# Two neighbouring weight rows to a partition, larger load pieces, and VectorE's extra jobs given out step by step, in an LSTM with a binary feed-forward net

## The chip, the cores and the metric

The kernel runs on one core of one Trainium2 chip. The metric is device time in microseconds; a run's time is taken around the whole execution. The profile shows one execution, by engine: TensorE (PE, with PEld for its weight loads), VectorE (DVE), ScalarE (ACT), GpSimd (POOL), SyncE (SP), and the DMA queues.

## The reference

x is 32 x 64 x 256 (sequences, steps, features), `cond` is 32 x 256, all f32. An LSTM runs over the 64 steps, a net with weights of +1 and -1 follows, and x is added:

```python
xW = jnp.einsum('ntd,dg->ntg', x, Wx) + b          # Wx 256 x 1024
a = xw_t + prev_h @ Wh                             # Wh 256 x 1024, one step
i, f, o = sigmoid(a[:, :256]), sigmoid(a[:, 256:512]), sigmoid(a[:, 512:768])
g = tanh(a[:, 768:])
next_c = f * prev_c + i * g
next_h = o * tanh(next_c)
# over all steps: hs, then, with w(k) = where(k, 1, -1)
h = relu(s0 * concat([hs, -hs]) @ w(k0)) * 2       # k0 512 x 1024
h = relu(s1 * h @ w(k1)) * 2                       # k1 1024 x 1024
out = x + s2 * h @ w(k2)                           # k2 1024 x 256
```

## The kernel before

**Layout.** The 256 hidden units are cut into four quarters q of 64. A partition holds (q, n): quarter q of sequence n, 4 x 32 = 128 partitions, so that the cell's elementwise work is 64 wide. Matmuls contract over 128 rows and take a step's x or h turned, 32 columns of sequences; their outputs go to the four quarters of the partitions, and four such matmuls run side by side. The 256 rows of Wx, Wh and of each half of k0 are two chunks of 128 partitions: row (q, b, j) lies in partition (q, j) of chunk b, j from 0 to 31. To match it, a transposition by 32 x 32 blocks on VectorE turns x (`turn_x`, line 214) and h (line 311).

**x products.** `x_part` (228 to 237) computes for one step and chunk the x share of the gates, and `x_products` (254) does two steps to a PSUM bank: eight calls of four matmuls each, and each f32 matmul is two matmul instructions in the profile. `evict_x` (242) adds the bias on VectorE and stores the bank to `xg`. `next_x` (247) turns the next eight steps of x and asks for the load of eight steps further on. The first eight steps are done in pieces, as their data come in, then steps 8 to AHEAD - 1 (here 12), and only then step 0 of the recurrence.

**A step** (lines 477 to 495): `gates_from_h` (273) multiplies h by Wh; `cell_step` (291) does the sigmoids and tanh on ScalarE and `kept`, `new`, `c`, `h` and the transposition to `hist` on VectorE, and copies the next step's `xg` into PSUM (ScalarE, 288 and 289). Behind that in program order come a step's share of other PE work and the chores. Each engine works in the order of the program. In steps 0 to X_STEPS - 1 (0 to 20) the PE work is x products, afterwards the feed-forward net of blocks of 16 steps (`ffn_block`, 373), shared evenly by a `goal`. The chores, one a step from step FIRST_CHORE (4) on, make the +1/-1 weights: four of `make_w0` (ScalarE and then VectorE, 190), eight of `make_w1` (ScalarE, 198), four of `make_w2` (ScalarE, 202). After every fourth step `split_h` (316) splits four steps' h into a high and a low part, on ScalarE (`hhi`) and VectorE (`hlo`).

**Loads.** SyncE and ScalarE share the first loads, in this order: four steps of x, Wx for f and o (chunk 0, then chunk 1), four steps of x, Wx for g, Wx for i, eight steps of x (half 1), Wh for g, Wh for i, f and o. Each is cut into four transfers of 32 partitions, two to a queue (`load_gates`, 109). Behind them SyncE alone loads x halves 2 and 3, k0 (eight transfers), k1 and further x. GpSimd loads the bias, `cond` and the scales.

Of the kernel before, what the change touches and what calls it, by code (L numbers as in the profile page):

```python
# [38 lines left out]
def lstm_ffn(ctx: ExitStack, tc: tile.TileContext, x, cond, wx_d, wh_d, b_d, k0_d, k1_d, k2_d, s0_d, s1_d, s2_d, out):  # L39
    nc = tc.nc  # L40
    P = 128
    N, T, D = x.shape
    H = cond.shape[1]
    G = 4 * H
    NQ = 4
# [4 lines left out]
    SB = 16  # L50
    NB = T // SB
    TB = SB * N
    SH = 4

    GATES = (3, 0, 1, 2)

    AHEAD = 12
    X_STEPS = 21

    FIRST_CHORE = 4  # L60
    WARM_UP = 8

    const = ctx.enter_context(tc.tile_pool(name="const", bufs=1))
# [15 lines left out]
    xq = {}  # L79
# [26 lines left out]
    def rows(t, q):  # L106
        return t[q * 32 : (q + 1) * 32]

    def load_gates(t, w_d, slots, engines, chunks=slice(0, 2)):

        w_rows = w_d.rearrange("(q b j) g -> q j b g", q=NQ, b=2)
        s0, n, g0 = slots[0], len(slots), GATES[slots[0]]
        for q in range(NQ):
            engines[q % len(engines)].dma_start(
                out=rows(t, q)[:, chunks, s0 * H : (s0 + n) * H],
                in_=w_rows[q, :, chunks, g0 * H : (g0 + n) * H],
            )

    load_x(0, 0, [nc.sync, nc.scalar], slice(0, SB // 4))
# [15 lines left out]
    h_first = const.tile([P, HQ], F32, name="h_first")  # L135
    nc.gpsimd.dma_start(out=h_first, in_=cond.rearrange("n (q j) -> q n j", q=NQ))
    scales = []
    for i, s_d in enumerate((s0_d, s1_d, s2_d)):
        s = const.tile([P, 1], F32, name=f"s{i}")
# [2 lines left out]
    load_x(1, 0, [nc.sync])  # L142
    load_x(1, 1, [nc.sync])

    k0_rows = k0_d.rearrange("(s q b j) g -> s q j b g", s=2, q=NQ, b=2)
    k0_bits = []
    for i in range(2):
        t = act([P, 2, F0], U8, f"k0_{i}")
        for q in range(NQ):
            nc.sync.dma_start(out=rows(t, q), in_=k0_rows[i, q])  # L150
        k0_bits.append(t)


# [48 lines left out]
    def make_w2(k, m):  # L202
        nc.scalar.activation(
            w2[:, m, ts(k, 4)].rearrange("p k (q j) -> p k q j", q=NQ),
            bits[FC0 + k].rearrange("p (k q m j) -> p m k q j", k=4, q=NQ, m=2)[:, m],
            AF.Identity,
            bias=minus1,
            scale=2.0,
        )


    xT = {}

    def turn_x(i, half, part=slice(0, SB // 2)):
        if part.start == 0:
            xT[i, half] = act([P, SB // 2, 2, N], F32, f"xT{i}_{half}")
        nc.vector.transpose(  # L217
            xT[i, half][:, part].rearrange("p t b n -> p (t b n)"),
            xq[i, half][:, part].rearrange("p t j -> p (t j)"),
        )  # L220

    wx_q = wx.rearrange("p k (g q j) -> p k q g j", g=4, q=NQ)
    wh_q = wh.rearrange("p k (g q j) -> p k q g j", g=4, q=NQ)
    xg = {}

    def x_part(p, t, k, slots, start):

# [14 lines left out]
    def evict_x(p, t):  # L242
        xg[t] = gpool.tile([P, 2, 4 * HQ], F32, tag="xg", name=f"xg{t}")
        b = bias[:, :4].rearrange("p g j -> p (g j)").unsqueeze(1).to_broadcast([P, 2, 4 * HQ])
        nc.vector.tensor_tensor(xg[t], p.rearrange("p t g j -> p t (g j)"), b, ALU.add)  # L245

    def next_x(half):

        if half < 2 * NB:
            turn_x(*divmod(half, 2))  # L250
            if half + 4 < 2 * NB:
                load_x(*divmod(half + 4, 2), [nc.sync])

    def x_products(t0, t1):

        for t in range(t0, t1, 2):
            p = x_bank(t)
            for s in range(2):
                for k in range(2):
                    x_part(p, t + s, k, slice(0, 4), s == 0 and k == 0)  # L260
                    if s == 1 and k == 1:
                        evict_x(p, t)
                        half, left = divmod(t + 2, SB // 2)
                        if left == SB // 4 and t + 2 != AHEAD:
                            next_x(half + 1)
                    yield 2


# [4 lines left out]
    def gates_from_h(t, hT):  # L273
        for g, slots in zip(gates, (slice(0, 3), slice(3, 4))):
            for k in range(2):
                for q in range(NQ):
                    nc.tensor.matmul(  # L277
                        g[q * N : (q + 1) * N],
                        hT[:, k, :],
                        wh_q[:, k, q, slots],  # L280
                        start=False,
                        stop=(k == 1),
                        skip_group_check=True,
                    )
# [6 lines left out]
    def cell_step(t, c):  # L291
        sig = cell.tile([P, 3, HQ], F32, tag="sig", name=f"sig{t}")
        cand = cell.tile([P, HQ], F32, tag="cand", name=f"cand{t}")
        nc.scalar.activation(sig[:, 0:2, :], gates[0][:, 1:3], AF.Sigmoid)  # L294
        nc.scalar.activation(cand, gates[0][:, 0], AF.Tanh)  # L295
        nc.scalar.activation(sig[:, 2, :], gates[1][:, 0], AF.Sigmoid)  # L296
        kept = cell.tile([P, HQ], F32, tag="kept", name=f"kept{t}")
        nc.vector.tensor_mul(kept, sig[:, 1, :], c)  # L298
        new = cell.tile([P, HQ], F32, tag="new", name=f"new{t}")
        nc.vector.tensor_mul(new, sig[:, 0, :], cand)  # L300
        c = cell.tile([P, HQ], F32, tag="c", name=f"c{t}")
        nc.vector.tensor_add(c, kept, new)  # L302
        th = cell.tile([P, HQ], F32, tag="th", name=f"th{t}")
        nc.scalar.activation(th, c, AF.Tanh)  # L304
        h = cell.tile([P, HQ], F32, tag="h", name=f"h{t}")
        nc.vector.tensor_mul(h, sig[:, 2, :], th)  # L306
        i, s = divmod(t, SH)
        if s == 0:
            hist[i] = hpool.tile([P, 2, SH * N], F32, tag="hist", name=f"hist{i}")
        hT = hist[i][:, :, ts(s, N)]  # L310
        nc.vector.transpose(hT, h.rearrange("p (b j) -> p b j", b=2))  # L311
        if t + 1 < T:
            gates_from_x(t + 1)
        return c, hT
# [135 lines left out]
    for t in range(SB // 2):  # L450
# [3 lines left out]
            evict_x(banks[t // 2], t - 1)  # L454
        if t == 1:
            turn_x(0, 1)
    nc.vector.transpose(hT, h_first.rearrange("p (b j) -> p b j", b=2))
    for _ in x_products(SB // 2, AHEAD):
        pass
    gates_from_x(0)  # L460
# [7 lines left out]
    chores = deque()  # L468
    chores += [lambda k=k, h=h: make_w0(k, h) for k in range(2) for h in range(2)]
    chores += [lambda k=k: make_w1(k) for k in range(FC0)]  # L470
    chores += [lambda k=k, m=m: make_w2(k, m) for k in range(2) for m in range(2)]

    work = x_products(AHEAD, T)
    total_x = (T - AHEAD) * 4
    total_ffn = (NB - 1) * (4 * FC0 + 2 * FC0 * FC1 + 4 * FC1)
    done = 0
    for t in range(T):
        gates_from_h(t, hT)
        c, hT = cell_step(t, c)
        if t == 0:  # L480
            next_x(AHEAD // (SB // 2) + 1)
        later = chores.popleft()() if t >= FIRST_CHORE and chores else None
        if outputs and next(outputs[0], "end") == "end":
            outputs.popleft()
        if t == X_STEPS:
            work, done = ffn(), 0
        goal = (t + 1) * total_x // X_STEPS if t < X_STEPS else (t + 1 - X_STEPS) * total_ffn // (T - X_STEPS)
        while done < goal:
            done += next(work)
        if t == X_STEPS - 1:  # L490
            next(work, None)
        if callable(later):
            later()
        if t % SH == SH - 1:
            split_h(t // SH)
    for n, _ in enumerate(work):
        if outputs and n % 4 == 0 and next(outputs[0], "end") == "end":
            outputs.popleft()
# [28 lines left out]
```

## Time and profile before

| what | value |
|---|---|
| median of four runs | 319.12 us (318.32 to 319.89) |
| the profiled execution's own time | 319.49 us |
| its span, from the first to the last instruction | 317.7 us |
| mean granted TensorE clock | 0.998 |
| start of the gate matmuls of step 0 | 19.58 us |
| start of the gate matmuls of step 21 | 84.00 us |
| an x turn, 128x512 (line 217) | 698 ns |
| an eviction of x products, 128x512 (line 245) | 662 ns |
| the product h, 128x64 (line 306) | 226 ns |
| h turned to hist, 128x64 (line 311) | 246 ns |

The page of a profile gives each engine's busy time, the span in 40 slices, and the chain of work that ended last, followed back from the end. The timeline merges neighbouring instructions of a kind: the columns are start, length, engine, line, operation, output <- input, count, and in brackets the idle time before with what ended it. A wait for several semaphores is put down to the one that came last by the profile. SPq and ACTq are transfers issued by SyncE and ScalarE; their rows show the issue, not the transfer.

### The profile page before, as it was taken

Reading aid. Unit: us, or ns where it says so; the run is one execution under the profiler, and the core shown is the slowest. Engines: PE = TensorE matmul, PEld = TensorE weight load, DVE = VectorE, ACT = ScalarE, POOL = GpSimd, SP = SyncE. Lnnn points to the kernel's source line nnn. Section 1 sums busy time; section 2 is a strip of 40 time slices with the busy share of each in tenths; the row PEclk is TensorE's granted clock in tenths of the full one; section 3 lists DMA queues with packets and bytes.
Section 4 is the critical chain, followed back from the end, with each engine's and each line's share of the span. In section 5 each row is a group of like instructions: output and inputs, shape, how many; then the busy total and the mean of one; then the engine's idle time right before and its main releaser. Section 6 shows DMA issues by size and latency. Waiting matters only on the chain.

```text
span 317.7 us, 9440 instructions
## 1 busy us (share of the span) xinstructions
PE 307.2 (97%) x3978; PEld 235.1 (74%) x3978; DVE 153.7 (48%) x473; ACT 130.8 (41%) x484; POOL 9.2 (3%) x28
## 2 busy tenths in 40 slices
PE   7889999999999999999999999999999999999992
PEld 4767777777877777777777777777777777888881
DVE  1355886756674433335745434467443433811114
ACT  0214567875563433344633334355334432511111
POOL 4400000000000000000000000000000000000001
PEclk9999999999999999999999999999999999999999
DMA  5665401142000000000010000001310000220002
GB/s 142 180 134 152 89 2 42 46 110 47 5 0 2 2 0 2 3 0 2 2 34 23 14 1 2 2 0 32 71 34 3 2 0 2 66 66 2 0 0 66
DMA packets 31001, 10.99 MB, mean 35 GB/s; under 512 B 28072, under 2 KB 30376, under 8 KB 30960
## 3 DMA queue, kind: packets, MB, share of 16 engines
q1 hardware_dynamic: 27648, 8.66, 11.3%
q10 hardware_dynamic: 3040, 1.57, 1.9%
q8 instruction: 31, 0.51, 0.7%
q0 software_dynamic: 272, 0.17, 0.3%
q14 instruction: 10, 0.08, 0.1%
HBM read 8.29 MB, written 2.10 MB: 33 GB/s over the span
## 4 chain that ended last, share of the span: by engine, by line
PE 88%; DMA 6%; DVE 3%; issue 1%; ACT 1%; DVEq 0%; ACTq 0%
PE p L407 38%; PE gates L277 19%; PE px L230 12%; PE p L379 10%; PE po L392 9%; DMA x<-in_x_dram 3%; DMA wx<-in_L_cond_Wx_dram 2%; DMA wh<-in_L_cond_Wh_dram 1%; DVE xg L245 1%; DVE w L194 0%; ACT th L304 0%; DVE h L306 0%; DVE c L302 0%; DVE o L362 0%; DVE hist L311 0%
## 5 line engine op out<-in xcount | busy, mean ns | idle before, releaser
L277 PEld LDWEIGHTS gates<-wh,hist 128*32 128x32 f32 x2016 | 54.3, 109 | 25.4 <-issue 14.1
L277 PE MATMUL gates<-wh,hist 128*32 128x192 f32 x2016 | 68.1, 275 | 0.4 <-DVE hist L311 0.3
L230 PE MATMUL px<-wx,xT 128*32 128x256 f32 (+1 forms) x1152 | 61.1, 357 | 1.5 <-DMA x<-in_x_dram 0.8
L294 ACT ACTIVATE sig<-gates 128x128 f32<-128x128 f32 x64 | 17.8, 278 | 81.4 <-PE gates L277 81.1
L230 PEld LDWEIGHTS px<-wx,xT 128*32 128x32 f32 x1152 | 40.2, 111 | 13.9 <-DVE xT L217 1.5
L298 DVE TENSOR_TENSOR kept<-sig,c 128x64 f32<-128x64 f32 x63 | 14.1, 224 | 59.5 <-ACT sig L294 59.2
L304 ACT ACTIVATE th<-c 128x64 f32<-128x64 f32 x64 | 16.5, 257 | 31.3 <-DVE c L302 31.3
L379 PE MATMUL p<-hhi,w 128*128 128x512 f32 x64 | 25.5, 399 | 0.0
L379 PE MATMUL p<-hlo,w 128*128 128x512 f32 x64 | 25.3, 395 | 0.0
L306 DVE TENSOR_TENSOR h<-sig,th 128x64 f32<-128x64 f32 x64 | 14.5, 226 | 20.7 <-ACT th L304 20.7
L245 DVE TENSOR_TENSOR xg<-px,bias 128x512 f32<-128x512 f32 x32 | 20.9, 662 | 5.1 <-POOL sgn L158 3.9
L288 ACT COPY gates<-xg 128x192 f32<-128x192 f32 x64 | 20.0, 313 | 0.0
L311 DVE STREAM_TRANSPOSE hist<-h 128x64 f32<-128x64 f32 x64 | 15.7, 246 | 2.4
L302 DVE TENSOR_TENSOR c<-kept,new 128x64 f32<-128x64 f32 x64 | 14.4, 225 | 2.2
L296 ACT ACTIVATE sig<-gates 128x64 f32<-128x64 f32 x64 | 14.9, 232 | 0.0
L379 PEld LDWEIGHTS p<-hhi,w 128*128 128x128 f32 x64 | 12.0, 188 | 2.8
L300 DVE TENSOR_TENSOR new<-sig,cand 128x64 f32<-128x64 f32 x64 | 14.0, 218 | 0.0
L295 ACT ACTIVATE cand<-gates 128x64 f32<-128x64 f32 x64 | 14.0, 218 | 0.0
L379 PEld LDWEIGHTS p<-hlo,w 128*128 128x128 f32 x64 | 12.0, 188 | 2.6
L407 PE MATMUL p<-a_7h,w 128*128 128x512 f32 x32 | 13.0, 407 | 0.0
L289 ACT COPY gates<-xg 128x64 f32<-128x64 f32 x64 | 13.0, 203 | 0.0
L407 PE MATMUL p<-a_2l,w 128*128 128x512 f32 x32 | 12.9, 403 | 0.0
(121 smaller groups left out, 500.0 us busy)
## 6 DMA issues: line engine op xcount, KB each, us to landing
x<-in_x_dram SPq DMA_DIRECT2D x58, 64.0 KB, 2.5
out_dram<-o SPq DMA_DIRECT2D x28, 64.0 KB, 1.8
bits<-in_L_ffn_k_dram SPq DMA_DIRECT2D x10, 128.0 KB, 2.3
wx<-in_L_cond_Wx_dram SPq DMA_DIRECT2D x8, 64.0 KB, 2.5
wx<-in_L_cond_Wx_dram ACTq DMA_DIRECT2D x8, 64.0 KB, 2.8
k<-in_L_ffn_k_dram SPq DMA_DIRECT2D x8, 64.0 KB, 3.0
wh<-in_L_cond_Wh_dram SPq DMA_DIRECT2D x2, 192.0 KB, 4.1
wh<-in_L_cond_Wh_dram ACTq DMA_DIRECT2D x2, 192.0 KB, 5.1
```

The lines of the kernel that those rows point to most:

```text
L230: nc.tensor.matmul(p[q * N : (q + 1) * N, t % 2, slots], xT[i // 2, i % 2][:, s, k, :], wx_q[:, k, q, slots], start=start, stop=False, ski ...
L245: nc.vector.tensor_tensor(xg[t], p.rearrange("p t g j -> p t (g j)"), b, ALU.add)
L277: nc.tensor.matmul(g[q * N : (q + 1) * N], hT[:, k, :], wh_q[:, k, q, slots], start=False, stop=(k == 1), skip_group_check=True,)
L288: nc.scalar.copy(gates[0], x_t[:, :3])
L294: nc.scalar.activation(sig[:, 0:2, :], gates[0][:, 1:3], AF.Sigmoid)
L296: nc.scalar.activation(sig[:, 2, :], gates[1][:, 0], AF.Sigmoid)
L304: nc.scalar.activation(th, c, AF.Tanh)
L306: nc.vector.tensor_mul(h, sig[:, 2, :], th)
L311: nc.vector.transpose(hT, h.rearrange("p (b j) -> p b j", b=2))
L379: nc.tensor.matmul(p, w0[:, k, ts(m, P)], a[:, k, :], start=(n == 0), stop=(n == 3))
L392: nc.tensor.matmul(po[m], w2[:, m, k], a1[k][n], start=(k == 0 and n == 0), stop=(k == FC1 - 1 and n == 1))
L407: nc.tensor.matmul(p1[m], w1[:, k, ts(m, P)], a0[k][n], start=(k == 0 and n == 0), stop=(k == FC0 - 1 and n == 1),)
```

## The change

- A partition holds two neighbouring rows: row 2p + b of Wx, Wh and of each half of k0 lies in partition p of chunk b. x and h are turned to match: `turn_x` reads every second of 64 elements, and `h` is written with its even elements first, then the odd ones.
- `load_gates` issues two transfers of 64 partitions in place of four of 32. k0 comes in two transfers in place of eight.
- AHEAD goes from 12 to 10.
- The chores begin in step 2. `make_w2` begins in step 24. VectorE's extra jobs (an x turn, a `split_h`, the VectorE half of `make_w0`) are held in queues; a step takes them while `load` (its evictions and turns so far) is under two, or when they are due. In a step with a `split_h` no chore is done.

```diff
-    AHEAD = 12
+    AHEAD = 10
     X_STEPS = 21
-    FIRST_CHORE = 4
+    FIRST_CHORE = 2
+    W2_STEP = 24
...
     def load_gates(t, w_d, slots, engines, chunks=slice(0, 2)):
-        w_rows = w_d.rearrange("(q b j) g -> q j b g", q=NQ, b=2)
+        w_rows = w_d.rearrange("(p b) g -> p b g", b=2)
         s0, n, g0 = slots[0], len(slots), GATES[slots[0]]
-        for q in range(NQ):
-            engines[q % len(engines)].dma_start(
-                out=rows(t, q)[:, chunks, s0 * H : (s0 + n) * H],
-                in_=w_rows[q, :, chunks, g0 * H : (g0 + n) * H],
+        for engine, half in zip(engines, (slice(0, P // 2), slice(P // 2, P))):
+            engine.dma_start(
+                out=t[half, chunks, s0 * H : (s0 + n) * H], in_=w_rows[half, chunks, g0 * H : (g0 + n) * H]
             )
...
-    k0_rows = k0_d.rearrange("(s q b j) g -> s q j b g", s=2, q=NQ, b=2)
+    k0_rows = k0_d.rearrange("(s p b) g -> s p b g", s=2, b=2)
...
-        for q in range(NQ):
-            nc.sync.dma_start(out=rows(t, q), in_=k0_rows[i, q])
+        nc.sync.dma_start(out=t, in_=k0_rows[i])
...
         nc.vector.transpose(
-            xT[i, half][:, part].rearrange("p t b n -> p (t b n)"),
-            xq[i, half][:, part].rearrange("p t j -> p (t j)"),
+            xT[i, half][:, part], xq[i, half][:, part].rearrange("p t (j b) -> p t b j", b=2)
         )
...
+    load = [0]
+    turns = deque()
...
+        load[0] += 1
         nc.vector.tensor_tensor(xg[t], p.rearrange("p t g j -> p t (g j)"), b, ALU.add)
...
         if half < 2 * NB:
+            load[0] += 1
             turn_x(*divmod(half, 2))
...
-                        if left == SB // 4 and t + 2 != AHEAD:
-                            next_x(half + 1)
+                        if left == 2 and half + 1 < 2 * NB:
+                            turns.append(half + 1)
+                        if left == 6 and turns:
+                            next_x(turns.popleft())
...
-        nc.vector.tensor_mul(h, sig[:, 2, :], th)
+        nc.vector.tensor_mul(
+            h.rearrange("p (b j) -> p j b", b=2),
+            sig[:, 2, :].rearrange("p (j b) -> p j b", b=2),
+            th.rearrange("p (j b) -> p j b", b=2),
+        )
...
-    nc.vector.transpose(hT, h_first.rearrange("p (b j) -> p b j", b=2))
+    nc.vector.transpose(hT, h_first.rearrange("p (j b) -> p b j", b=2))
...
-    chores += [lambda k=k, m=m: make_w2(k, m) for k in range(2) for m in range(2)]
+    chores2 = deque(lambda k=k, m=m: make_w2(k, m) for k in range(2) for m in range(2))
+    splits, w0_parts = deque(), deque()
...
     for t in range(T):
+        load[0] = 0
         gates_from_h(t, hT)
         c, hT = cell_step(t, c)
-        if t == 0:
-            next_x(AHEAD // (SB // 2) + 1)
-        later = chores.popleft()() if t >= FIRST_CHORE and chores else None
+        if t % SH == SH - 1:
+            splits.append(t // SH)
...
-        if callable(later):
-            later()
-        if t % SH == SH - 1:
-            split_h(t // SH)
+
+        if turns and load[0] < 2:
+            next_x(turns.popleft())
+        if splits and (load[0] < 2 or t >= X_STEPS or t == SH * splits[0] + 2 * SH - 1):
+            split_h(splits.popleft())
+        else:
+            if t >= FIRST_CHORE and chores:
+                part = chores.popleft()()
+                if part is not None:
+                    w0_parts.append(part)
+            elif t >= W2_STEP and chores2:
+                chores2.popleft()()
+            if w0_parts and (load[0] < 2 or t == X_STEPS - 1):
+                w0_parts.popleft()()
```

## Prediction

> **What bounds the kernel now.** I read the page first: its busy shares, its chain and the DMA row in 40 slices.
>
> ```profile
> span 317.7 us, 9440 instructions
> PE 307.2 (97%) x3978; PEld 235.1 (74%) x3978; DVE 153.7 (48%) x473; ACT 130.8 (41%) x484; POOL 9.2 (3%) x28
> DMA  5665401142000000000010000001310000220002
> ```
>
> TensorE (PE) is busy for 97% of the span, and the change takes none of its work away. So a gain can only come out of PE's idle time. I looked for that stage by stage, by the start of each step's gate matmuls (line 277, the timeline): step 0 starts at 19.58 us, step 21 (the first with feed-forward work) at 84.00. From there to the last step every period is 4.18 or 4.41 us without a gap. What is left is the stretch before 19.58 and the 21 steps that carry the x products. The chain of waits, cut to the first 26 us, tells what the first stretch waits for:
>
> ```profile
> 0.74 1.98 DMA x<-in_x_dram
> 2.74 3.22 DMA wx<-in_L_cond_Wx_dram
> 5.99 2.11 DMA wx<-in_L_cond_Wx_dram
> 8.11 4.94 DMA x<-in_x_dram
> 13.08 4.69 DMA wh<-in_L_cond_Wh_dram
> 17.78 1.82 DMA x<-in_x_dram
> 19.60 1.06 PE gates L277 x32
> ```
>
> Each transfer starts 0.02 to 0.03 us after the one above it has landed. That is no data dependence: the built order shows that an issue on SyncE or ScalarE waits for the landing of the transfer four places earlier on its queue. So a queue has four pieces in flight, and the large wh pieces (192 KB) stand in the fifth round. The last row's name misleads: what released step 0 is the last wh piece, issued on ScalarE's queue at 13.69. The view of the tile wh gives
>
> ```profile
> DMA to landing us min/median/max: 2.9/4.8/5.5
> ```
>
> so it lands at 13.69 + 5.5 = 19.2, 0.4 before the gates. The busy table by stretches shows what the rounds cost:
>
> ```profile
> core 0: us, PE busy (x) PEld busy (x) DVE busy (x) ACT busy (x) POOL busy (x), PEclk, DMA share, GB/s
> 9.00:11.00 2.00, 1.25 (x48) 1.01 (x44) 0.00 (x0) 0.00 (x0) 0.30 (x1) 1.00 0.81 180
> 11.00:14.00 3.00, 3.00 (x116) 3.00 (x112) 0.83 (x2) 0.00 (x0) 1.20 (x6) 1.00 0.34 103
> 14.00:18.00 4.00, 3.85 (x86) 2.69 (x76) 3.19 (x6) 1.84 (x4) 1.17 (x8) 1.00 1.05 236
> ```
>
> From 11 to 14 us the DMA engines stand at a share of 0.34 because the next pieces may not be issued; as soon as wh may go, they are full (1.05).
>
> In the x steps a plain period is 3.03 us: 0.87 for the gates and five groups of eight x matmuls at 0.432 (2.16). Step 10 has four groups, 2.60 us of PE work, yet takes 2.88: that is the recurrence itself (gates, sigmoid, cell, transpose). So the recurrence has 0.15 us to spare in a plain x step and 1.3 us in a feed-forward step. Steps 4 and 8 take 3.31 and 3.52. In the timeline of VectorE (DVE) ahead of the latter:
>
> ```profile
> 43.71 0.24 DVE L311 STREAM_TRANSPOSE hist<-h 128x64 f32<-128x64 f32 x1
> 43.88 1.25 DVE L245 TENSOR_TENSOR xg<-px,bias 128x512 f32<-128x512 f32 x2
> 45.05 0.73 DVE L194 SCALAR_TENSOR_TENSOR w<-k,nsgn,w0t 128x512 fp32r<-128x512 uint8 x1
> 45.70 0.42 DVE L327 TENSOR_TENSOR hlo<-hist,hhi 128x256 fp32r<-128x256 f32 x1
> 46.04 0.22 DVE L298 TENSOR_TENSOR kept<-sig,c 128x64 f32<-128x64 f32 x1
> ```
>
> Four extra jobs stand ahead of `kept`, whose input was ready 0.65 us earlier (sig started at 45.08, and `kept` follows that by 0.31 in a plain step). PE waits for 0.49 of it.
>
> **The change part by part.**
>
> Pieces of wx and wh. Eighteen transfers a queue up to wh become twelve, in the order x, x, wx, wx, x, x, wx, wx, x, x, wh, wh. The last wh piece (now 384 KB) waits for the wx piece of gate i, that one for the second piece (chunk 1) of f and o, and that one for nothing: three rounds in place of five. Rounds: the free piece is issued at about 2.1 us (before, the fourth of its queue went at 2.10 and 2.16). Its size doubles, 64 KB more, some 0.4 us at half the 300 KB/us that both queues move together (before, 301 KB in the best microsecond). With the chain's 3.22 for such a piece 3.6; the next one 2.9 (before, 2.1 to 3.2) and 0.4, 3.3; wh 5.3 (before up to 5.5, at a full 1.05). Sum 14.3, and 0.4 to the gates: 14.7. By engine time: share times length over 1.0 to 19.5 us is about 12.9 us, near 12 without the later x pieces; at a share of 0.9 from 1.5 us on it ends at 14.8, gates at 15.2. I take 14.9. Below, PE bounds it: its first x matmul needs the first x and wx pieces (5.23 now), and the work ahead of step 0 is 256 half-width matmuls at 27 ns and, after the change, 32 at 54 (64 now): 8.64 us, so not before 13.87. Above, 19.58 as now.
>
> The Trainium skill, SBUF — State Buffer, "Door 1: The DMA port swizzle", speaks against such pieces: 64 partitions reach no more ports than 32 and were measured only 4% faster, 196 GB/s. At 196 GB/s the some 2.75 MB up to wh would need 14.0 us and gates would start near 15.9, a microsecond after my value. The row from 14 to 18 us, with two queues at once on 32-partition pieces, moved 236 GB/s, so I don't use it.
>
> AHEAD 12 to 10. One bank of x products, 32 matmuls, 1.73 us, moves from before step 0 into the steps, where PE has no room: it is paid in full. The x steps hold 108 groups in place of 104. Three steps get six groups (3.46 us), the other eighteen five: 3 x 3.46 + 18 x 3.03 = 64.92 us. The four-group step and its 0.29 idle go.
>
> VectorE's extra jobs. The order after shows at most two extra jobs in any x step but the last, where a third (0.74) runs into a feed-forward step with its 1.3 us of room. The idle of 0.28, 0.49 and small 0.04 goes; the 0.13 of step 18, whose cause I don't see, I keep. Two jobs fit: in a step with an x turn the last bank of x products ends 0.43 us before the next gates at the latest, the eviction (0.65) follows some 0.2 behind it and then the turn (0.69), so DVE is free 1.12 us after the gates' start, and `kept` comes at 1.27 to 1.29.
>
> Strided DVE access. No row of before has it. h is the 128x64 row (226 ns), the x turn the 128x512 row (698 ns). Low end: nothing, since the transposes h to hist (246) and h_first (223), whose shapes differ from the x turn's only in length, scale with elements; a gain has no reason, since no element goes away. High end for h: the 128x512 eviction's 662 ns, as if each element cost eight; for the turn, its per-element part doubled, (698 - 445)/256 = 0.99 ns, +0.5 us. The rows nearest, other 64-element operations at 218 to 246 ns, speak for the low end; I take zero, and up to 0.15 us more on h is free in any case.
>
> The same page and section say that an access which crosses to a new 16-byte line pays a penalty; by it a stride of two f32 is free, and h, written 128 bytes apart, pays at every element, with no size given. No row here shows it.
>
> The rest costs nothing. k0 in two pieces of 256 KB: issued once x half 2 has landed, near 16 us, wanted at the end of step 2, near 23.5. The x half 2 itself is wanted by DVE at 14.9 + 2.73 + 0.65 = 18.3; its issue waits for x half 1 and, as now, stands behind wh on SyncE's ring (now 14.29 to 19.9, 5.6 us; after, from about 11 on). If it comes late, DVE stands still in front of `kept`, and each microsecond beyond 18.3 is lost. make_w2 (four times 0.72 on ScalarE) moves from steps 16 to 19 to steps 24 to 28, where ScalarE waits over 2.5 us for each sigmoid; its first reader, line 392, comes in step 27.
>
> Sum. Step 21 starts at 14.9 + 64.92 + 0.13 = 79.95 in place of 84.00: 4.05 us less. Behind it all is PE work as before. The profiled execution took 319.49 (span 317.7 and 1.8 around it), so 315.4 for it; it lies 0.37 over the median of the four runs, 319.12, and the forecast for a median is 315.1.
>
> **The rivals.**
> - Bytes bind more than rounds. Pieces of 256-byte packets run at a DMA share of 0.7 or so (5 to 9 us: 0.64), and the instruction fetches hold single engines back; then wh lands around 16.6, gates at 17.0: 319.12 - 1.95 = 317.2. For: the 4.94 us of the x piece in the chain. Against: that piece ended in the stretch at 0.34.
> - The load doesn't come sooner at all (the change misses its end): gates at 19.58, and the 1.73 moved behind them weighs against 1.10 of idle that goes: +0.63, 319.75.
> - Other side: the strided accesses are dear. h at 0.65 us is 0.27 over the spare 0.15 in 21 x steps, 5.8; x turns six times 0.11 beyond their room (0.65 + 1.2 - 1.6 - 0.15), 0.7, and 0.25 ahead of step 0: together 6.75, 321.8. It decides from h at about 0.57 us on, (0.57 - 0.226 - 0.15) x 21 = 4.05. In feed-forward steps it stays hidden. Against: all 64-element DVE rows.
>
> **How the numbers follow.** Forecast 0.64, bytes 0.20, no sooner 0.07, strides 0.06, the rest (a late x half 2, something unseen) 0.03. The range: PE's bound 13.87 gives 314.0, less 0.8 for the runs' own spread (318.32 to 319.89), 313.2; above, the bytes rival and 0.7, 317.9. Some 0.5% is what a measurement of this kernel tells from none. Under 317.5: the forecast and most of the bytes rival, 0.82; over 320.7: strides, 0.06; between, 0.12.
>
> **What would show it.** Right: gates of step 0 between 14 and 16 us, no DMA slice near 0.1 ahead of them, plain x steps of 3.03 and three of 3.46, none between; h near 226 ns. Wrong: wh landing after 17, h over 0.38 us, DVE waiting for x half 2, or a feed-forward period over 4.41.

## The result and the profile after

| what | before | after |
|---|---|---|
| median of the runs | 319.05 us (317.92 to 321.48, 71 runs) | 319.40 us (318.35 to 321.58, 45 runs) |
| ratio after to before, 95% interval | | 1.0013 [1.0003, 1.0024] |
| the profiled execution's own time | 319.49 us | 319.34 us |
| gate matmuls of step 0 | 19.58 us | 18.04 us |
| gate matmuls of step 21 | 84.00 us | 83.68 us |
| from step 0 to step 21 | 64.42 us | 65.64 us |

The change made no gain: 319.4 us in place of the 315.1 forecast. Three lines of the page of after answer to those of before:

```profile
span 317.5 us, 9412 instructions
PE 307.2 (97%) x3978; PEld 237.2 (75%) x3978; DVE 157.3 (50%) x473; ACT 131.0 (41%) x484; POOL 9.2 (3%) x28
DMA  5775101043000000000011000001310000220002
```

PE is as busy as before, VectorE 3.6 us busier, and the first slices of the DMA row (7.9 us each) read 5775 in place of 5665: the load has hardly been drawn forward. The chain of waits of after, cut to the first 20 us (start, length, what):

```profile
2.27 4.36 DMA wx<-in_L_cond_Wx_dram
...
6.66 3.35 DMA wx<-in_L_cond_Wx_dram
...
10.03 7.76 DMA wh<-in_L_cond_Wh_dram
...
18.04 1.08 PE gates L282 x32
```

Three rounds stand where five stood, as forecast, and wh is asked for at 10.03 in place of 13.69. But it takes 7.76 us to land. The timeline of TensorE in that stretch shows what the wait costs:

```profile
8.56 7.43 PE L231 MATMUL px<-wx,xT 128*32 128x128 f32 x224 [0.57 <-DVE xT L216]
18.04 1.08 PE L282 MATMUL gates<-wh,hT_first 128*32 128x192 f32 x32 [2.04 <-DMA wh<-in_L_cond_Wh_dram]
```

The x products end at 16.0, and PE then stands idle for 2.04 us. The same three stretches as in the prediction's busy table (DMA share and GB/s are the last two columns):

```profile
core 0: us, PE busy (x) PEld busy (x) DVE busy (x) ACT busy (x) POOL busy (x), PEclk, DMA share, GB/s
9.00:11.00 2.00, 2.00 (x82) 2.00 (x78) 0.00 (x0) 0.40 (x1) 0.99 (x2) 1.00 0.95 233
11.00:14.00 3.00, 3.00 (x114) 2.87 (x107) 1.62 (x3) 1.56 (x4) 1.07 (x6) 1.00 0.48 114
14.00:18.00 4.00, 2.00 (x41) 1.34 (x33) 2.39 (x5) 0.00 (x0) 1.30 (x8) 1.00 1.11 242
```

The hole from 11 to 14 us, which the prediction put down to the rounds, is still there (0.48), though every piece of wh has been issued by 10.03. So there is a second cause, and it is this hole that the experiments look for first.

The step times of after are 3.27, 3.14, 3.03, 3.46, 3.03, 3.36 for steps 0 to 5, and then 3.03, with 3.46 in steps 10 and 17: the three six-group steps are as forecast, but steps 0, 1 and 5 are late by 0.24, 0.11 and 0.33.

### The profile page after: what moved, and what is told of

It reads as the page before. It is cut to its first block, busy times and chain, and to the rows that moved or that the text cites. A ratio compares the mean times of both kernels' runs of the same rounds, so it can differ in the third digit from the quotient of the medians.

```text
span 317.5 us, 9412 instructions
## 1 busy us (share of the span) xinstructions
PE 307.2 (97%) x3978; PEld 237.2 (75%) x3978; DVE 157.3 (50%) x473; ACT 131.0 (41%) x484; POOL 9.2 (3%) x28
## 3 DMA queue, kind: packets, MB, share of 16 engines
q1 hardware_dynamic: 27200, 8.66, 11.3%
q10 hardware_dynamic: 2944, 1.57, 2.0%
## 4 chain that ended last, share of the span: by engine, by line
PE 91%; DMA 5%; DVE 1%; ACT 1%; issue 1%; ACTq 0%; DVEq 0%
PE p L416 38%; PE gates L282 19%; PE px L231 14%; PE p L388 10%; PE po L401 9%; DMA wh<-in_L_cond_Wh_dram 2%; DMA wx<-in_L_cond_Wx_dram 2%; DVE o L371 0%; ACTq L87 0%; DVE a_7l L342 0%; ACT sig L299 0%; ACTq L115 0%; DVE o L379 0%; ACT th L309 0%; DVE c L307 0%
## 5 line engine op out<-in xcount | busy, mean ns | idle before, releaser
L282 PE MATMUL gates<-wh,hist 128*32 128x192 f32 x2016 | 68.8, 275 | 0.0
L231 PE MATMUL px<-wx,xT 128*32 128x256 f32 (+1 forms) x1152 | 62.2, 359 | 0.8 <-DVE xT L216 0.6
L231 PEld LDWEIGHTS px<-wx,xT 128*32 128x32 f32 x1152 | 42.4, 112 | 11.9 <-DVE xT L216 1.9
L311 DVE TENSOR_TENSOR h<-sig,th 128x64 f32<-128x64 f32 x64 | 17.7, 277 | 20.7 <-ACT th L309 20.7
L307 DVE TENSOR_TENSOR c<-kept,new 128x64 f32<-128x64 f32 x64 | 14.4, 225 | 2.2
```

The costliest lines, as they stand in the source:

```text
L231: nc.tensor.matmul(p[q * N : (q + 1) * N, t % 2, slots], xT[i // 2, i % 2][:, s, k, :], wx_q[:, k, q, slots], start=start, stop=False, ski ...
L282: nc.tensor.matmul(g[q * N : (q + 1) * N], hT[:, k, :], wh_q[:, k, q, slots], start=False, stop=(k == 1), skip_group_check=True,)
L311: nc.vector.tensor_mul(h.rearrange("p (b j) -> p j b", b=2), sig[:, 2, :].rearrange("p (j b) -> p j b", b=2), th.rearrange("p (j b) -> p j ...
```

## The experiments

The theory after the result: the rounds went as forecast, and the load is late for two other reasons, a stall of the DMA engines near 11 to 13.5 us and a low rate of pieces that cover half of the partitions; with AHEAD of 10, work was moved behind step 0 out of a place where TensorE then idled. The rivals: TensorE's instruction fetch makes the hole; the strided accesses cost time; the spread jobs cost time. Each kernel is after with one edit, unless it is said otherwise. "Step 0" and "step 21" are the starts of their gate matmuls in the profiled execution, "ratio" is to the kernel before on the same chip. The profiled executions of e1, e2 and e6 took 0.8, 1.1 and 1.0 us longer than their medians, so there the ratio tells more than the steps.

| kernel | median us | ratio, 95% interval | step 0 | step 21 | between |
|---|---|---|---|---|---|
| e1_ahead12 | 318.23 | 0.9976 [0.9960, 0.9991] | 18.63 | 83.43 | 64.80 |
| e2_wh_128_partitions | 318.31 | 0.9977 [0.9959, 0.9996] | 18.12 | 83.87 | 65.75 |
| e3_scales_later | 318.00 | 0.9973 [0.9958, 0.9987] | 16.88 | 82.06 | 65.18 |
| e5_before_scales_later | 318.97 | 1.0004 [0.9986, 1.0023] | 19.07 | 83.51 | 64.44 |
| e6_wh128_scales_later | 317.50 | 0.9959 [0.9944, 0.9974] | 17.67 | 83.03 | 65.36 |
| e7_h_unstrided | 319.29 | 1.0027 [1.0002, 1.0051] | 17.80 | 83.45 | 65.65 |
| e8_spread_undone | 319.92 | 1.0033 [1.0014, 1.0052] | 18.23 | 84.42 | 66.19 |
| e9_pieces_undone | 320.73 | 1.0062 [1.0040, 1.0084] | 20.29 | 85.35 | 65.06 |
| e10_scales_later_ahead12 | 317.12 | 0.9936 [0.9916, 0.9956] | 17.67 | 81.69 | 64.02 |
| e11_act_four_more | 317.81 (one run) | | 17.43 | 82.39 | 64.96 |
| e12_all_gates_128 | 316.19 | 0.9912 [0.9887, 0.9937] | 15.42 | 80.42 | 65.00 |
| e13_all_gates_128_scales_kept | 317.33 | 0.9946 [0.9925, 0.9967] | 15.51 | 81.70 | 66.19 |
| e14_before_gates_128 | 330.03 | 1.0341 [1.0309, 1.0374] | 27.16 | 93.72 | 66.56 |

**What makes the hole.** e4 keeps the loads alone; matmuls, cell and net are left out.

> The loads of the changed kernel alone: all matmuls, the cell and the net are left out, and wh is copied to the output. Only the head is read. Theory A (the scales' tiny transfers make the half-empty stretch): the last wh piece still lands near 17.8 us. Theory B (the instruction fetch for TensorE's matmuls makes it): there is no fetch now, wh data flow from 11.5 us on, and the last piece lands near 15. Theory C (the wh transfers' own flow at 219 KB/us): the flow of the last 768 KB takes 3.5 us in either case.

```profile
11.00:13.00 2.00, 0.00 (x0) 1.25 (x2) 0.82 (x4) 1.00 0.46 136
```

This is the busy table of e4 (no PE column, as PE runs nothing). The share is 0.46 (in after, 0.50 from 11 to 13 us) with no instruction of TensorE to fetch, and wh lands at 17.78: the fetch isn't the hole's cause. e3 takes the three scale loads away from there and puts them behind k0:

```diff
-        nc.gpsimd.dma_start(out=s, in_=s_d.partition_broadcast(P))
...
+    for s, s_d in zip(scales, (s0_d, s1_d, s2_d)):
+        nc.sync.dma_start(out=s, in_=s_d.partition_broadcast(P))
```

> The changed kernel with the loads of the three scales (128 descriptors of 4 bytes each, issued by GpSimd at 8.3 to 10.0 us) moved behind k0 on SyncE's queue. Theory A (these tiny writes hold up the DMA engines from 10.5 to 13.5 us, and wh behind them): wh data flow from 11.5 us on, the last piece lands near 15.5, step 0 starts near 16.0, when TensorE is done with its x products, and the time is 2 us less. Theory B (the stretch has another cause: the instruction fetch of 16 KB at 10.3, or the descriptors of wh themselves): step 0 stays within 0.5 us of 18.0.

```profile
11.00:14.00 3.00, 3.00 (x111) 2.82 (x107) 2.24 (x4) 1.77 (x4) 0.00 (x0) 1.00 1.02 253
```

Its busy table has no hole: 1.02 and 253 GB/s where after has 0.48 and 114. wh lands at 16.63, step 0 starts at 16.88. That is the landing of theory A in direction, but 1.1 us later than it said. So it was the scale loads, three transfers of 512 bytes in pieces of 4 bytes, issued by GpSimd at 8.33 to 9.45 us, ahead of the large wh pieces, that held the engines up. In the trace of after their packets, 48 of 32 bytes, run from 10.23 to 13.54 us, as long as the hole lasts. How they hold the others up isn't seen: each of them takes only 13 to 36 ns. The same edit in the kernel before:

> The kernel before with one edit: the three scale loads moved from GpSimd to SyncE's queue behind k0. Theory (the tiny transfers held single DMA engines up in the kernel before as well; its eight-step x pieces had 15 of 16 engines done at 10.95 to 12.5 us and the last at 12.86 to 13.67, and the large wh pieces waited for just that): x lands near 11.5, wh is issued 1.5 us earlier, and step 0 starts when TensorE is done with its x products, 18.4 to 18.6 in place of 19.58: about 1 us less than before. Rival (in the kernel before, the instruction fetch at 10.8 us is what holds that engine up): wh is issued at 12.9 as before and nothing changes.

It brought nothing that can be measured (1.0004), though its profiled execution has step 0 at 19.07, 0.5 earlier, and the share from 11 to 14 us rises from 0.34 to 0.69. So the scale loads made a part of the hole of before too, and what is left is put down to the rounds of four, which stand there as before: the last wh piece is issued at 12.78 in place of 13.69. The microsecond expected was not borne out.

**The rate of the pieces.** e2 cuts wh by chunk over 128 partitions, so that the rule for half of the partitions, which the prediction cites, no longer applies to it:

```diff
-    load_gates(wh, wh_d, (0,), [nc.sync, nc.scalar])
-    load_gates(wh, wh_d, (1, 2, 3), [nc.sync, nc.scalar])
+    for cols, src in ((slice(0, H), slice(3 * H, 4 * H)), (slice(H, 4 * H), slice(0, 3 * H))):
+        for k, engine in enumerate((nc.sync, nc.scalar)):
+            engine.dma_start(out=wh[:, k, cols], in_=wh_rows[:, k, src])
```

> The changed kernel with wh cut by chunk and not by half of the partitions: each wh transfer covers all 128 partitions, SyncE's chunk 0 and ScalarE's chunk 1. Bytes and number of transfers are the same. Theory A (the 768 KB of the last two wh pieces flow at 219 KB/us, 14.2 to 17.7 us, because a transfer to 64 partitions has half the way into the memory): packets of 3072 bytes take nearer 120 ns than 230, the 768 KB flow in about 2.4 us, step 0 starts near 17. Theory B (what counts is the stretch from 10.5 to 13.5 us in which the DMA engines are half empty although wh is issued): that stretch stays, and step 0 moves by under 0.5 us.

A packet of 3,072 bytes took 125 ns on the mean, in after 209. But the hole stayed (0.57 from 11 to 14 us). Fifteen of the sixteen engines had landed their part at 16.27, the last one at 18.21, and step 0 stayed at 18.12, as theory B has it. In the medians e2 is better than after all the same (0.9977 to 1.0013). TensorE had a new idle stretch:

```profile
13.51 3.23 PE L233 MATMUL px<-wx,xT 128*32 128x128 f32 x77 [0.69 <-issue]
```

"Issue" means that nothing that the profile shows held it. e6 makes both edits, e3's and e2's:

> The changed kernel with both edits, wh cut by chunk over 128 partitions and the scales behind k0. Theory: the half-empty stretch is gone and wh packets take 121 ns, so the last wh piece lands by 15 us, ahead of TensorE, which is done with its x products near 16.1: step 0 near 16.1 to 16.4, step 21 near 81.3, the time 1.5 to 2.3 us under the changed kernel's and 0.4 to 0.8 under that with the scales alone. Rival (one DMA engine is held up by something else, such as the instruction fetch): the last of the 16 engines lands after 16.5 and nothing is gained over the scales alone.

```profile
14.81 3.23 PE L234 MATMUL px<-wx,xT 128*32 128x128 f32 x77 [1.85 <-issue]
```

The hole is gone, but the idle of "issue" grew to 1.85, and the last of the sixteen engines landed its part of wh at 17.68, where fifteen had at 15.85: the rival is what the profile shows. The trace has instruction packets of 16 KB on a queue of their own; in e6 one began at 10.63 and took 2.87 us, where the others of this stretch take 0.9 to 1.6. TensorE went on 1.31 us after its end. That is hardly chance: in after, e1, e2 (twice), e7, e8 and e13 (three times) an idle stretch of TensorE's matmuls or weight loads ends 1.47 to 1.55 us after the end of such a packet, in e10 twice at 1.7 to 1.8. In e4, where TensorE runs nothing, that queue moves no packet, and the page of after counts its packets among those of the 16 DMA engines that carry the loads. So TensorE waits at times for its own instructions. No run changes that alone, so it is argued from the times; many such packets delay nothing (in e12 three fall into steps 0 to 4, and none of these steps is late).

e13 cuts all loads of gate rows, wx too, by chunk over 128 partitions, and leaves the scales; e12 moves the scales as well:

```diff
-        for engine, half in zip(engines, (slice(0, P // 2), slice(P // 2, P))):
-            engine.dma_start(
-                out=t[half, chunks, s0 * H : (s0 + n) * H], in_=w_rows[half, chunks, g0 * H : (g0 + n) * H]
-            )
+        for k in range(chunks.start, chunks.stop):
+            engines[k].dma_start(
+                out=t[:, k, s0 * H : (s0 + n) * H], in_=w_rows[:, k, g0 * H : (g0 + n) * H]
+            )
```

> The kernel after with the scale loads behind k0, and every load of gate rows (wx and wh) cut by chunk over 128 partitions, chunk 0 on SyncE, chunk 1 on ScalarE. Theory A (the rate of the pieces binds: 121 ns a packet of 3072 bytes over 128 partitions, 220 to 250 over 64): wh lands before 15.5 us on 15 of 16 engines and step 0 starts at 15.0 to 16.5, TensorE's own work (13.9 at least) being next; time 0.993 to 0.996 of the kernel before. Theory B (the engine that carries TensorE's instruction fetch is then the last one: its fetch stands behind the loads' packets): TensorE waits 1 to 2 us for instructions ahead of step 0, which starts at 17.0 to 18.0, and the time is that of the kernel with wh alone over 128 partitions, 0.9959, or more.

> The kernel after with every load of gate rows cut by chunk over 128 partitions, and the three scale loads left where they are, on GpSimd. With both edits step 0 started at 15.2 to 15.4; with the scale loads moved alone at 16.9 to 17.5; with wh alone over 128 partitions at 18.1. Theory A (the scale loads hold the DMA engines up for some 1.5 us whatever the pieces): a hole at a share of 0.4 to 0.5 near 11 to 13 us is there again, wh lands at 16.3 to 17.5, step 0 starts at 16.8 to 17.8, ratio to the kernel before 0.994 to 0.998. Theory B (the cut over 128 partitions alone is what was missing; the early wx loads leave room for the scales): step 0 at 15.2 to 15.6, ratio 0.989 to 0.993.

The timeline of TensorE in e12 up to step 0, and the busy table from 11 to 14 us:

```profile
5.41 9.94 PE L232 MATMUL px<-wx,xT 128*32 128x128 f32 x288 [0.36 <-DMA wx<-in_L_cond_Wx_dram]
15.42 1.08 PE L283 MATMUL gates<-wh,hT_first 128*32 128x192 f32 x32
```

```profile
11.00:14.00 3.00, 3.00 (x102) 2.71 (x98) 2.77 (x5) 0.47 (x2) 0.00 (x0) 1.00 1.07 283
```

From 5.41 us on TensorE has no idle in front of step 0; wh lands at 14.94, before the x products end. The x steps take 65.00, all of them 3.03 or 3.46 but for 0.05 in step 5. This is what the prediction had for the change itself (14.9, 64.92 and 79.95; here 15.42, 65.00 and 80.42). At 316.19 us it is the best kernel of the study, 0.9% under before.

e13 reaches almost the same step 0 (15.51), with the scales where they were: the cut alone is enough there. The expected stall near 11 to 13 us didn't come (0.83 from 11 to 14 us), but a shorter one came later:

```profile
13.50:14.50 1.00, 1.00 (x37) 0.82 (x30) 0.82 (x2) 0.00 (x0) 0.00 (x0) 1.00 0.51 124
```

In e12 the share is 1.09 there. In e13 the last wh piece is issued at 8.66, ahead of all three scale loads (8.89 to 10.00), whose packets run from 12.43 to 14.72 us; in after the large wh pieces go behind them. So the stall seems to move with the scale loads, and here most of wh is already in: it lands at 15.33, in e12 at 14.94. But its steps 0 to 4 lose 1.1 us that e12 doesn't lose; nearly all of it is two idle stretches of TensorE's weight loads (0.43 and 0.59) that end 1.48 and 1.51 us behind instruction packets. Why those packets come later in e13 (15.39 and 20.54 us, the latter 1.57 long) than in e12 (13.84 and 19.62, 1.20 and 0.96 long) was not settled.

e9 undoes the pieces alone, four transfers of 32 partitions again:

```diff
-        for engine, half in zip(engines, (slice(0, P // 2), slice(P // 2, P))):
-            engine.dma_start(
-                out=t[half, chunks, s0 * H : (s0 + n) * H], in_=w_rows[half, chunks, g0 * H : (g0 + n) * H]
-            )
+        for q in range(NQ):
+            part = slice(q * 32, (q + 1) * 32)
+            engines[q % len(engines)].dma_start(
+                out=t[part, chunks, s0 * H : (s0 + n) * H], in_=w_rows[part, chunks, g0 * H : (g0 + n) * H]
+            )
```

> The kernel after with one thing undone: each load of gate rows is again cut into four transfers of 32 partitions, two to a queue (row pairs, turns, AHEAD of 10 and the spread jobs stay). Theory A (the rounds of four are real, larger pieces brought wh forward): wh is issued near 13.7 us again (after: 9.8 to 10.0), lands near 19.2, and step 0 starts at 19.2 to 19.6 in place of 18.0; x steps 65.0 to 65.6; step 21 at 84.4 to 85.1, so 0.9 to 1.5 us over the kernel after, a ratio of 1.003 to 1.006 to the kernel before. Theory B (the pieces bring nothing, the scales and the rate set wh's landing whatever the pieces): step 0 at 17.9 to 18.3 and the time of the kernel after, 1.0013.

Theory A: 1.0062 against 1.0013, so larger pieces are worth about half a per cent. Step 0 came later still than expected, 20.29, because the hole hit two wx pieces (issued at 8.11 and 8.45, landed at 13.05 and 13.40), and TensorE stood still for them, 3.42 us in all:

```profile
13.64 6.84 PE L232 MATMUL px<-wx,xT 128*32 128x128 f32 x160 [3.42 <-DMA wh<-in_L_cond_Wh_dram]
```

(The releaser named is not the one; the matmuls behind the idle read wx.) From 13.2 to 16.6 us the granted clock was 0.50, so the products ahead of step 0 took longer too; in after it stayed at 1.00 through 2.04 us of idle.

```profile
14.00:16.00 2.00, 2.00 (x47) 2.00 (x42) 0.31 (x1) 0.69 (x1) 1.00 (x7) 0.50 0.70 184
```

So the half per cent holds for these loads as they stand, this loss of clock included.

e14 is the kernel before, with its rows, turns, AHEAD and jobs, in which the gate rows are loaded by chunk over 128 partitions and the scales behind k0:

```diff
-        for q in range(NQ):
-            engines[q % len(engines)].dma_start(
-                out=rows(t, q)[:, chunks, s0 * H : (s0 + n) * H],
-                in_=w_rows[q, :, chunks, g0 * H : (g0 + n) * H],
-            )
+        for k in range(chunks.start, chunks.stop):
+            engines[k].dma_start(
+                out=t[:, k, s0 * H : (s0 + n) * H], in_=w_rows[:, :, k, g0 * H : (g0 + n) * H]
+            )
```

> The kernel before, with its rows, turns, AHEAD of 12 and jobs, in which only the loads differ: gate rows cut by chunk over 128 partitions, and the scale loads behind k0. Theory A (what pays is how the loads are cut and what runs beside them; neither the row pairs nor AHEAD of 10 is needed): TensorE runs without a gap from 5.4 us on, 9.9 us as with row pairs and 1.73 for the bank more, so step 0 starts at 17.0 to 17.4; the x steps take 64.4 as before, step 21 starts at 81.4 to 81.9 (before 84.0), ratio 0.991 to 0.995. Theory B (row pairs are needed for the rate): step 0 at 18.5 or later, ratio 0.997 or more.

Theory A is out. Theory B's bounds hold, but it said nothing of this size: 3.4% slower, with step 0 at 27.16 and 5.24 us long. Its busy table:

```profile
4.00:10.00 6.00, 1.98 (x23) 1.10 (x25) 0.45 (x1) 0.00 (x0) 0.54 (x2) 1.00 0.35 113
10.00:20.00 10.00, 8.35 (x225) 7.30 (x221) 2.30 (x5) 1.84 (x4) 0.41 (x1) 1.00 0.45 130
```

The engines are a third to a half busy, at 113 to 130 GB/s, and the trace shows why: for 6.5 of the 8.1 us in which its 3,072-byte packets run, four of them are in flight, in e12 up to sixteen and more. A row (q, b, j) of one chunk lies in four blocks of 32 rows, so the transfer's outer dimension has four entries, and four engines carry it; TensorE's long waits for them cost clock as well (0.50 from 27.6 to 31.0 us). With two neighbouring rows to a partition the outer dimension is the 128 partitions. The Trainium skill, DMA: Bandwidth & Descriptors, section "Why a DMA increments its semaphore by 16 and not by 1", states this rule (the number of engines follows from the slowest dimension of the access patterns), and e14 agrees, with its four packets in flight. So row pairs have a part in the gain of e12 after all, as what lets this cut over 128 partitions run on all engines. Another way of cutting the old rows was not tried.

**The bank moved behind step 0.** e1 is after with `AHEAD = 12`, e10 is e3 with it.

> The changed kernel with AHEAD back at 12, all else kept. Theory (in the changed kernel TensorE is done with its x products at 16.0 us and waits until 18.0 for the last wh piece, so the bank of 1.73 us that was moved behind step 0 had a free place ahead of it): step 0 stays at 18.0 us, the x steps hold 104 groups of eight matmuls in place of 108, step 21 starts near 82.1 in place of 83.57, and the time is about 1.4 us less than the changed kernel, near 318.0. Rival (the extra bank ahead of step 0 slows the loads or comes too late itself): step 0 moves to 19 or later and nothing is gained.

> The kernel after with the three scale loads behind k0 on SyncE, and AHEAD of 12. With AHEAD of 10 this order had PE's x products done at 16.2 and step 0 at 16.8 to 16.9, so only 0.67 us of PE idle ahead of it. Theory A (TensorE sets the end, idle ahead of step 0 is the only free place): 1.73 us of products go ahead of step 0, which starts at 17.9 to 18.1; the x steps get a four-group step and no six-group one, 63.6 to 63.9 in all; step 21 at 81.6 to 81.9 in place of 81.98, so within 0.4 us of the kernel with AHEAD of 10, ratio to the kernel before 0.995 to 0.998. Theory B (AHEAD of 10 is the better choice once wh lands early, as PE has nothing idle): no better or up to 0.7 us worse, if the fetch of PE's instructions falls into the gates of step 0 as it did with AHEAD of 12 alone (idle of 0.70 there).

e1 is 0.4% better than after (0.9976 to 1.0013), e10 than e3 (0.9936 to 0.9973). As long as TensorE waits for wh, a bank of products ahead of step 0 is partly free. In the profiled execution of e1 the gain is smaller than the 2.04 us of idle would allow, since its step 0 takes 3.89:

```profile
20.20 0.37 PE L282 MATMUL gates<-wh,hT_first 128*32 128x64 f32 x12 [0.70 <-issue]
```

an instruction packet began only at 17.52 and ended at 18.70, 1.50 before TensorE went on. In e10 step 0 started at 17.67 and no such idle fell into its gates; its profile is 0.37 us ahead of e3's at step 21, less than the ratios say.

**VectorE: the spread, and the strides.** e8 has after's loads and turns, and the chores, turns and splits where before had them.

> The changed kernel with the chores, x turns and splits ordered as before (first chore in step 4, each at once), and all else kept. Theory (the spreading took VectorE's pile-ups away, which cost 0.28 and 0.49 us in steps 4 and 8 of the kernel before): in steps 4 and 8 or their neighbours 0.3 to 0.5 us come back, and the time is 0.5 to 0.8 us over the changed kernel's. Rival (spreading brought nothing: the six-group steps give the same cover): no step but those of six groups is over 3.1, and the time is the same.

The x steps take 66.19 in place of 65.64, 0.55 us more, as expected, though the intervals of the two ratios overlap (1.0033 and 1.0013). The pile-up is in step 7, 0.73 late: in VectorE's timeline two evictions, a turn and a part of `make_w0` stand ahead of `kept`. The rest of the difference is not the spread: step 2 of e8 is late by 0.39 behind an instruction packet, and steps 0, 1 and 5 by 0.6 less than in after. e7 writes h in order, as before (its units then don't match the rows of Wh, which changes nothing in the amount of work):

> The changed kernel with h written in the order of the kernel before (so the units of h no longer match the rows of wh and w0). Theory (h's 277 ns in place of 226 lies inside the 0.15 us that the recurrence has to spare in an x step): h takes 226 ns, plain x steps stay at 3.03 us and the time stays within 0.3 us of the changed kernel's. Rival (the longer h makes the x steps 1 and 5 late): these lose their 0.1 and 0.33 us, and the time falls by 0.4 us or more.

The groups of the page of after, and the view of the tile h of e7 (min, median and max in ns):

```profile
L311 DVE TENSOR_TENSOR h<-sig,th 128x64 f32<-128x64 f32 x64 | 17.7, 277 | 20.7 <-ACT th L309 20.7
```

```profile
L311 DVE TENSOR_TENSOR h<-sig,th x64: 224/226/227, 20.0 to 264.9; 128x64 f32<-128x64 f32 x64
```

The stride costs h 51 ns (226 to 277), inside the 0.15 us that were free; the x turn stayed at 0.69 to 0.70 us. Plain x steps are 3.03 in both, and e7's time isn't better than after's.

**What makes step 5 late.** In after, the gates of step 5 start at 33.98, and its first sigmoid comes 1.42 us later, where a plain step has 0.97 to 1.08:

```profile
33.54 0.72 ACT L192 ACTIVATE w0t<-k,sgn 128x512 f32<-128x512 uint8 x1
35.40 0.28 ACT L299 ACTIVATE sig<-gates 128x128 f32<-128x128 f32 x1 [1.14 <-PE gates L282]
```

An instruction packet of 8 KB, of another queue than TensorE's, runs from 34.88 to 35.39. If it is ScalarE's, it must come after a fixed number of ScalarE's instructions. e11 is e3 with four more one-element sigmoids in an idle stretch of ScalarE:

```diff
     nc.scalar.activation(warm[:, 1:2], warm[:, :1], AF.Sigmoid)
+    for n in range(4):
+        nc.scalar.activation(warm[:, n + 2 : n + 3], warm[:, :1], AF.Sigmoid)
```

> The kernel after with the scale loads behind k0, and four more one-element sigmoids on ScalarE behind its first one, near 12 us, where it stands idle until 17.8. It tests what makes step 5 late by 0.2 to 0.3 us in each kernel with the new order. Theory A (ScalarE's own instruction fetch: a packet of 8 KB at 33.26, 0.55 us long, just where step 5's first sigmoid is due; it comes after a fixed number of ScalarE instructions): the fetch comes four instructions earlier, about two thirds of a step; step 5 takes 3.03, and step 4 may take 3.03 to 3.5. Theory B (something else of step 5, as VectorE's turn or a load): step 5 stays at 3.2 to 3.4 and step 4 at 3.03.

Theory A, in the one run that there is: the packet comes at 32.24 (e3: 33.26), step 5 takes 3.03, and step 4 too; no x step is late any more. The first sigmoid of its step 5 starts 0.97 us after the gates' start at 33.02:

```profile
33.99 0.28 ACT L302 ACTIVATE sig<-gates 128x128 f32<-128x128 f32 x1 [0.80 <-PE gates L285]
```

## Why the prediction was wrong

**Where it failed.** The step is the term for the last wh piece: "wh 5.3 (before up to 5.5, at a full 1.05)". It took over the time of a 192 KB piece for one of 384 KB that is issued 3.7 us earlier, and it measured 7.76. The terms of the sum, forecast and measured in the chain of after:

| term | forecast | measured |
|---|---|---|
| the free wx piece is issued | 2.1 | 2.27 |
| its time to land | 3.6 | 4.36 |
| the second | 3.3 | 3.35 |
| wh | 5.3 | 7.76 |
| to the gates | 0.4 | 0.24 |
| sum, with 0.06 of issue | 14.7 | 18.04 |

Of the 3.3 us that are missing wh has 2.5 and the first piece 0.8. The busy tables from the issue of the last wh piece to its landing, of before, after and e3, show what it waits for:

```profile
13.69:19.18 5.49, 4.55 (x98) 3.00 (x87) 4.01 (x7) 1.84 (x4) 1.40 (x9) 1.00 0.89 202
```

```profile
10.03:17.80 7.77, 5.97 (x180) 5.18 (x168) 4.02 (x7) 1.96 (x4) 2.37 (x13) 1.00 0.83 190
```

```profile
10.24:16.63 6.39, 5.86 (x166) 4.93 (x160) 3.80 (x7) 1.96 (x4) 0.00 (x0) 1.00 1.04 230
```

By an estimate, length times rate, some 1.1 MB were moved in that time in before, but 1.5 MB in after and in e3: a piece that is asked for earlier has more of the other loads to share with. Without the scale loads ahead of it this takes 6.4 us (e3); the hole that they make adds 1.4. Those are the 2.5 us. Wider pieces did not shorten this term: in e12 the last wh piece takes 6.37 us too. But it is issued at 8.57, since the wx pieces ahead of it landed sooner, at a DMA share of 0.93 from 2 to 9 us (e3: 0.70), and so step 0 starts 2.5 to 2.6 us earlier in e13 and e12 than in after. Why the share is higher there was not taken apart.

**The bound below.** The prediction let TensorE's work end no sooner than 13.87, with 8.64 us from 27 ns for each half-width matmul and 54 for each full one. In e12, where TensorE has no idle, that work takes 9.94 us: the first 32 matmuls take 1.66 us, each 32 of the next ones 0.88, and the trace's first record of the clock, 1.00, begins at 7.04 us, about where those 32 end. So 14.9 lay below the 15.35 at which TensorE is done in e12.

**The row that led astray.** The hole at a share of 0.34 in before was put down wholly to pieces that may not be issued. e5 shows that it has two causes at the same place: with the scale loads moved the share there is 0.69. GpSimd's six busy instructions in that row, the scales' arithmetic as their loads landed, were in plain view.

**The rule that was set aside.** The prediction held 236 GB/s of the stretch from 14 to 18 us against the Trainium skill's 196 GB/s (SBUF — State Buffer, "Door 1: The DMA port swizzle"), and left the rule out. The rate itself was not so wrong: after moves 242 GB/s there. The page's figure is too low for this case: from 13.4 to 14.4 us after moves 270 GB/s, nearly all of it SyncE's one piece over 64 partitions. But the page's direction holds: over 128 partitions e2 moves 328 GB/s from 13 to 15 us, and a packet takes 125 ns for 209. The row of before was one of small partition spans at a share of 1.05, so it left no room for more of the same. The page's section "Can I just issue two DMAs to hit both halves?" says that two transfers at partitions 0 and 64 gain only 6% over one; that is the form of this change. No run times one half alone, but e13, with step 0 at 15.51 for 18.04, agrees that a span of 128 is the better one. The rule alone gave 15.9 us for step 0, 2 us less than came, the hole being no part of it.

**AHEAD.** "Paid in full" was right for the x steps: the three six-group steps took 3.46, and e1 and e10 show about 0.4% for the bank. What it missed is the other side: with TensorE idle for 2.04 us ahead of step 0, the bank could have stood there nearly free. With step 0 bound by TensorE, as in e12, it would be paid for; that was not run.

**Spread.** Right in the main: without it a pile-up of 0.73 us comes back (e8), and in after the idle of steps 4 and 8 is gone. But steps 0, 1 and 5 lost 0.68 in its place, which the prediction did not have: 0.35 to TensorE's instruction fetch, as argued above (idle up to 20.23, an instruction packet's end at 18.71), and 0.33 to ScalarE's. The 0.13 that was kept for step 18 did not come. So the x steps took 65.64 in place of 65.05.

**What held.** Three rounds in place of five; strides free; k0, x half 2 and `make_w2` free (the steps from 21 on are 4.18 and 4.41, as before). Of the rivals, "bytes bind more than rounds" named the right place, and its 16.6 for wh is close to what e3 shows (16.63); in after the stall of the scale loads, which it did not know, came on top. "Wrong: wh landing after 17" is what the profile shows: 17.80.

**The sum.** Head −1.54 (19.58 to 18.04), x steps +1.22, together −0.32 at step 21 and −0.2 in the span. In the medians even that is not seen (+0.35 us, 1.0013).

## What to carry to other kernels

A hole in the DMA share can have two causes at once, and one that is explained by order of issue should still be tried with the small loads of the same stretch taken away. Time a piece that is asked for earlier by all the bytes that have to land with it, not by the row of a later and smaller one, and give weight loads a layout whose outer dimension is all 128 partitions before making them larger. And before work is moved from a wait into a full stretch, make sure that the wait is gone.

## What the runs showed of the hardware that was not expected

- Three transfers of 512 bytes in 4-byte pieces, issued by GpSimd, held the DMA engines up as long as their packets ran: the share from 11 to 14 us was 0.48 with them (after) and 1.02 without (e3). Issued behind the large loads they did so later and for less long (e13, 0.51 from 13.5 to 14.5 us).
- TensorE seems to wait for its own instructions: idle stretches of 0.3 to 1.9 us end 1.3 to 1.8 us after an instruction packet of 16 KB, which goes over the same DMA engines as the loads and took 0.9 to 2.9 us.
- A transfer over 128 partitions, whose rows come in four blocks, ran four packets at a time (113 to 130 GB/s) and made the kernel 3.4% slower.
- In an idle stretch of 3.42 us TensorE's granted clock went to 0.50 after 3.0 us and stayed there for 3.4 us (e9); through 2.04 us of idle it stayed at 1.00 (after).
- The start of step 0 differed by 0.55 us between two executions with the same loads (e3 16.88, e11 17.43).
